# Carrying a hand-made instruction order across the seam between two graph-attention layers

## The chip, the cores and the metric

The kernel runs on one core of one Trainium2 chip. The metric is the device time of one execution in microseconds (us). Before the change three timed runs gave 937.43, 938.22 and 939.72 us; their median is 938.22 us. The profile below comes from one further execution, of 938.49 us, whose profiled span is 936.6 us.

## The reference: what is computed

Two layers work on 4096 nodes with 512 features. `x` is (4096, 512), `adj` is (4096, 4096) with about one entry in some hundreds above zero. Each layer is a layer norm, a ReLU and an attention, added to its input. Layer 0 attends only inside blocks of 128 nodes; layer 1 attends over all edges, with eight heads.

```python
# layer 0: attention inside each graph of 128 nodes, biased by adj
h = jnp.maximum(_layernorm(x), 0.0)
query, key, value = h @ Wq.T + bq, h @ Wk.T + bk, h @ Wv.T + bv
a = jnp.where(mask, query @ key.T * scale, 0.0)
scores = (a + adj + adj) * jnp.where(mask, 1.0, -1000000.0)
x = x + (jax.nn.softmax(scores, axis=-1) * mask) @ value

# layer 1: every node attends over its neighbours, 8 heads of 64
h = jnp.maximum(_layernorm(x), 0.0)
mx = jnp.einsum('nf,hfd->hnd', h, W)
logits = s_i[:, :, None] + t_j[:, None, :]      # s = mx.a_origin, t = mx.a_dst
attn = jax.nn.softmax(jnp.where(adj[None] > 0, logits, neg_inf), axis=-1)
x = x + concat_heads(einsum('hij,hjd->hid', attn, mx))
```

The kernel works on 32 row tiles of 128 nodes. It has three stages. Stage one is layer 0: 16 iterations of two row tiles each, `g = 0` to `15`. Stage two, the part between the layers, finishes for every row tile `i` the layer norm and ReLU of layer 1, turns the tile (features to partitions), multiplies it with `W` and weighs it with `exp(t)`; the result is `parts[i]`. Part of this is already done inside stage one: row tiles 0 to 7 are projected there, and row tiles up to 15 are normed and turned there. Stage three is layer 1's aggregation, one long product of the 0/1 mask with the 32 parts for each of 32 row tiles.

## The kernel before

The constants that matter are `NT = 32` row tiles, `G = 2` tiles an iteration, `NG = 16` iterations, `LO = 8`, `AHEAD = 10`, `BY = 4` row tiles in a chunk, and `KC = 4`. A "chunk" of four row tiles is turned in two steps: the vector engine transposes blocks of 32 by 32 into a buffer `blocks`, the buffer is stored to memory (`store`), and it is read back with the features on the partitions (`move`). The buffers of the helpers' results come from pools with a fixed number of buffers; `ps_p` has four PSUM buffers, and every projection takes two of them.

The helpers of one row tile `i` of layer 1 are these:

```python
def moments(src):                                    # two DVE and two POOL operations
    nc.vector.bn_stats(stats, src)
    nc.vector.bn_aggr(mv, stats)
    nc.gpsimd.tensor_scalar(ve, mv[:, 1:2], EPS, None, ALU.add)
    nc.gpsimd.tensor_tensor(rstd, ve, neghalf, ALU.pow)
    return mv[:, 0:1], rstd

def norm(src, hn, of=None):                          # one DVE operation
    mean, rstd = of or moments(src)
    nc.vector.tensor_scalar(hn, src, mean, rstd, ALU.subtract, ALU.mult)

def turn(i, row, pool):                              # one DVE operation
    c, b = divmod(i, BY)
    if b == 0:
        blocks[c] = pool.tile([P, P // B, KC, BY, B], F32, name="blocks")
    nc.vector.transpose(blocks[c][:, :, :, b], ...)

def store(c):                                        # 1 MB to memory
    nc.sync.dma_start(hT_d[c], ...blocks[c]...)

def move(c):                                         # 1 MB back, four DMAs
    hT = keep.tile(..., tag="a" if c and c % 2 == 0 else "hT4")
    for q in range(P // B):
        nc.sync.dma_start(hT[ts(q, B)]..., hT_d[c, :, q]...)

def fetch(i):                                        # pool sb2 has two of these buffers
    rows[i] = sb2.tile([P, D], F32, name="row1")
    nc.sync.dma_start(rows[i], x1_d[i])

def relu1(i):
    norm(rows[i], rows[i], of[i])
    nc.scalar.activation(rows[i], rows[i], AF.Relu)

def project1(ps_m, hT, w1x):                         # 16 matmul records, two PSUM buffers
    pm = [ps_m.tile([P, D], F32, name="pp") for _ in range(2)]
    for g, n in ((1, HW + H), (0, HW)):
        for k in range(KC):
            nc.tensor.matmul(pm[g][:, :n], hT[:, k, :], w1x[:, k, ...], ...)
    return pm

def prepare():
    i = len(parts)
    pm = project1(ps_p, hTs[i], w1x)
    e = weights(i, pm)                               # exp on ACT, two small POOL operations
    return lambda: finish(e, pm, part_tile(lo, i))   # two DVE products (weigh), a cast on ACT,
                                                     # a subtraction on POOL (split)
```

The end of an iteration of stage one, its last iteration and the part between the layers are as follows.

```python
with tc.manual_schedule(engines={E.PE, E.DVE, E.Activation, E.Pool, E.SP}):
    for g in range(NG - 1):
        mine = g - 1
        # ... loads, scores, queries, masks ...
        if g > 1:
            of[mine] = moments(rows[mine])
        if g:
            fetch(g)
        # ... values of the next pair ...
        attend(sT, vs[0], g, 0, lambda: nvs.append(v0()))   # a matmul, x1 = ... on DVE, x1 stored
        attend(sT, vs[1], g, 1)
        if g:
            relu1(mine)
        # ...
        nvs.append(values(nhT, 1))
        if g:
            turn(mine, rows[mine], keep)
        # ...

    g = NG - 1
    fetch(g)
    s = scores(hT, gT, rs[g], *look)
    rest = prepare()
    of[g - 1] = moments(rows[g - 1])
    row_sums(g, *look)
    relu1(g - 1)
    sT = turned(s)
    turn(g - 1, rows[g - 1], keep)
    rest()
    rest = prepare()
    of[g] = moments(rows[g])
    relu1(g)
    attend(sT, vs[0], g, 0)
    rest()
    rest = prepare()
    turn(g, rows[g], keep)
    store(LO // BY + 1)
    attend(sT, vs[1], g, 1)
    rest()

# ... pools of layer 0 closed, pools hi and sb4p opened ...

with tc.manual_schedule(engines={E.DVE, E.Activation, E.Pool, E.SP}):
    first = LO + AHEAD
    for i in range(2 * LO, first + 2):
        load(i)                                      # sb4, five buffers "row2"
    move(LO // BY + 1)
    for i in range(2 * LO, first):
        norm(rows[i], rows[i])
        nc.scalar.activation(rows[i], rows[i], AF.Relu)
        if i + 1 < first:
            turn(i, rows[i], keep)
    for i in range(LO, NT):
        far = i + AHEAD
        load(far + 2)
        if far % BY == 1 and LO + AHEAD < far <= NT + 1:
            move(far // BY - 1)
        # ... first mask of stage three, near the end ...
        low()
        if far < NT:
            of[far] = moments(rows[far])
        if far <= NT:
            turn(far - 1, rows[far - 1], ...)
            if far % BY == 0:
                store(far // BY - 1)
        pm = project1(ps_p, hTs[i], w1x)
        if before:
            low = finish(*before, later=True)
        if far < NT:
            norm(rows[far], rows[far], of[far])
        before = (weights(i, pm), pm, upper[i])
        if far < NT:
            nc.scalar.activation(rows[far], rows[far], AF.Relu)
```

Inside `manual_schedule` the named engines take their instructions in the order of the program. There are two such contexts here, one after the other, and the second does not name PE. Where the two meet, the framework's own scheduler decides how the instructions of one are mixed with those of the other: in the profile the loads of row tiles 16 to 19 stand on the queue at 325.81 us, ahead of `fetch(15)` at 335.57 us, which the program has first.

Of the kernel before, what the change touches and what calls it, by code (L numbers as in the profile page):

```python
# [9 lines left out]
F32 = mybir.dt.float32  # L10
# [43 lines left out]
def kernel(  # L54
# [332 lines left out]
    with ExitStack() as straight:  # L387
# [4 lines left out]
        with ExitStack() as prep:  # L392
# [26 lines left out]
            def store(c):  # L419
                nc.sync.dma_start(hT_d[c], blocks[c].rearrange("p q k b r -> p q (k b r)"))  # L420
# [13 lines left out]

            rows, of = {}, {}

            def fetch(i):
                rows[i] = sb2.tile([P, D], F32, name="row1")
                nc.sync.dma_start(rows[i], x1_d[i])

            def relu1(i):
# [22 lines left out]
            with (  # L464
# [90 lines left out]
                def store_mask(i):  # L555
                    nc.sync.dma_start(a_d[i], a8s[i].bitcast(F32))
# [9 lines left out]
                def seen():  # L566
                    return (
                        sb.tile([P, G, P], F32, name="diag"),
                        [small.tile([P, 4], F32, name="sums", bufs=8) for _ in range(G)],
                        [],  # L570
                    )
# [45 lines left out]
                def load_pair(g):  # L617
                    xg[g] = sb.tile([P, G, D], F32, name="xg", bufs=3)
                    nc.sync.dma_start(
                        xg[g], x[g * G * P : (g + 1) * G * P, :].rearrange("(t p) d -> p t d", p=P)  # L620
                    )
# [35 lines left out]


                E = mybir.EngineType
                with tc.manual_schedule(engines={E.PE, E.DVE, E.Activation, E.Pool, E.SP}):  # L660
                    for g in range(NG - 1):
                        new = G * (g + 1)
                        mine = g - 1
                        if g + 2 < NG:
                            load_pair(g + 2)
                        if g in (5, 9, 13):
                            store(g // BY - 1)
                        if g == 1:
                            fetch(0)
                            w1x, dots = load_w1(pool1, sb2, tag="e")  # L670
                        if g in (6, 11, 14):
                            move((6, 11, 14).index(g))
                        nlook = seen()

                        def look_on(t, h):
                            sum_half(new + t, h, nlook[0][:, t, :], nlook[1][t], nlook[2])

                        def between(m):
                            if m < 2:
                                mask_half(new, m)  # L680
                                look_on(0, m)
                            if m == 1:
                                store_mask(new)
                                row_sums(g, *look)
                            if m > 1:
                                mask_half(new + 1, m - 2)

                        s = scores(hT, gT, rs[g], *look)
                        ngT = queries(nhT, between)
                        sT = turned(s)  # L690
                        if g + 2 < NG:
                            ofs = [moments(xg[g + 2][:, t, :]) for t in range(G)]
                        look_on(1, 0)
                        rest = prepare() if g in (7, 8, 9, 10, 13) else None
                        look_on(1, 1)
                        store_mask(new + 1)
                        if g > 1:
                            of[mine] = moments(rows[mine])
                        if g:
                            fetch(g)  # L700
                        if g + 2 < NG:
                            hns = normed0(g + 2, ofs)
                        if 2 <= g < 2 + KC:
                            dots(g - 2)
                        v0 = values(nhT, 0, later=True)
                        nvs = []
                        if rest:
                            rest()
                        attend(sT, vs[0], g, 0, lambda: nvs.append(v0()))
                        attend(sT, vs[1], g, 1)  # L710
                        if g == 1:
                            of[0] = moments(rows[0])
                        if g:
                            relu1(mine)
                        if g + 2 < NG:
                            rs[g + 2] = row_terms(hns)
                        nvs.append(values(nhT, 1))
                        if g:
                            turn(mine, rows[mine], keep)
                        hT, gT, vs, look = nhT, ngT, nvs, nlook  # L720
                        if g + 2 < NG:
                            nhT, hns = turned0(g + 2, hns)


                    g = NG - 1
                    fetch(g)
                    s = scores(hT, gT, rs[g], *look)
                    rest = prepare()
                    of[g - 1] = moments(rows[g - 1])
                    row_sums(g, *look)  # L730
                    relu1(g - 1)
                    sT = turned(s)
                    turn(g - 1, rows[g - 1], keep)
                    rest()
                    rest = prepare()
                    of[g] = moments(rows[g])
                    relu1(g)
                    attend(sT, vs[0], g, 0)
                    rest()
                    rest = prepare()  # L740
                    turn(g, rows[g], keep)
                    store(LO // BY + 1)
                    attend(sT, vs[1], g, 1)
                    rest()

# [11 lines left out]
                    rows[i] = sb4.tile([P, D], F32, name="row2", bufs=5)  # L759
                    nc.sync.dma_start(rows[i], x1_d[i])  # L760

            E = mybir.EngineType
            with tc.manual_schedule(engines={E.DVE, E.Activation, E.Pool, E.SP}):
                first = LO + AHEAD
                for i in range(2 * LO, first + 2):
                    load(i)
                move(LO // BY + 1)
                for i in range(2 * LO, first):
                    norm(rows[i], rows[i])
                    nc.scalar.activation(rows[i], rows[i], AF.Relu)  # L770
                    if i + 1 < first:
                        turn(i, rows[i], keep)
                before = None
                low = lambda: None
                for i in range(LO, NT):
                    far = i + AHEAD
                    load(far + 2)
                    if far % BY == 1 and LO + AHEAD < far <= NT + 1:
                        move(far // BY - 1)
                    if far == NT + 1:  # L780
# [12 lines left out]
                    low()  # L793
                    if far < NT:
                        of[far] = moments(rows[far])
                    if far <= NT:
                        turn(far - 1, rows[far - 1], (keep, sb4)[(far - 1) // BY % 2])
                        if far % BY == 0:
                            store(far // BY - 1)
# [393 lines left out]
```

## Time and profile before

| what | from the page |
|---|---|
| span | 936.6 us |
| PE (matmul) busy | 922.0 us |
| DVE busy | 475.0 us |
| ACT busy | 261.4 us |
| POOL busy | 161.1 us |
| mean granted TensorE clock | 0.995 |
| stage one, from the first matmuls to the last scores | until about 336 us |
| part between the layers | about 336 to 442 us |
| stage three, aggregation | 442 us to the end |

PE stands for the matrix engine, DVE for the vector engine, ACT for the scalar engine, POOL for the general-purpose engine and SP for the queue engine that issues most transfers. A busy PE only says that matmuls are in flight. The boundaries of the stages are read from the chain of waits, in which the products of line 322 (stage three) start at 442.08 us and the last scores of line 578 at 334.20 us. Line 271 is the projection of the part between the layers, line 280 the weighing that frees its PSUM buffers, line 415 the block transpose of `turn`, line 420 the store of a chunk, line 428 its way back, line 612 the `x1` of layer 0's attention and line 760 the load of a row tile.

### The profile page before, as it was taken

How to read it: one execution, taken by the hardware profiler on the slowest of the kernel's cores; microseconds unless marked ns; L12 is line 12 of the kernel's file. 1: busy time of each engine (PE TensorE's matmuls, PEld its weight loads, DVE VectorE, ACT ScalarE, POOL GpSimd, SP SyncE). 2: the span in 40 equal slices, each digit the busy share in tenths (PEclk: the TensorE clock that was granted, in tenths of full speed). 3: DMA queues.
4: the chain of work that ended last, by engine and by line, in shares of the span. 5: the costliest groups of instructions: out<-in, count | busy, mean ns of one | idle time of the engine just before them, and what ended most of it. 6: DMA issues, size and time to landing. Idle time of an engine off the chain costs nothing.

```text
span 936.6 us, 13023 instructions
## 1 busy us (share of the span) xinstructions
PE 922.0 (98%) x4933; PEld 804.9 (86%) x4933; DVE 475.0 (51%) x1016; ACT 261.4 (28%) x507; POOL 161.1 (17%) x344
## 2 busy tenths in 40 slices
PE   8999999999999998999999999999999999999997
PEld 6776676767777666888999999999999999999997
DVE  5477888777677656645362424242423233232412
ACT  5476677655567633332000000000000000000000
POOL 2112111222211224554101011010101010101010
PEclk9999999999999998999999999999999999999999
DMA  9999999999899636762213131312222221312111
GB/s 340 409 330 390 367 378 363 366 377 350 307 346 366 211 131 173 222 177 66 68 46 91 46 91 51 85 51 85 54 82 69 68 86 50 90 46 91 45 45 37
DMA packets 63941, 165.01 MB, mean 176 GB/s; under 512 B 7042, under 2 KB 23810, under 8 KB 54658
## 3 DMA queue, kind: packets, MB, share of 16 engines
q1 hardware_dynamic: 54370, 147.35, 46.9%
q10 hardware_dynamic: 9504, 16.78, 4.7%
q8 instruction: 40, 0.66, 0.3%
q14 instruction: 27, 0.22, 0.1%
HBM read 122.16 MB, written 41.94 MB: 175 GB/s over the span
## 4 chain that ended last, share of the span: by engine, by line
PE 93%; DMA 3%; DVE 1%; POOL 1%; issue 0%; ACT 0%; SPq 0%; ACTq 0%; DVEq 0%
PE pg L322 51%; PE pp L504 12%; PE pp L517 12%; PE pp L271 8%; PE pss L578 3%; PE pp L609 3%; PE pt L135 1%; PE pp L242 1%; DMA row<-x_d 1%; PE pl L322 1%; DMA hT_d<-blocks 1%; DMA bk_sb<-bk 0%; POOL rstd L123 0%; PE pss L601 0%; DVE stats L117 0%
## 5 line engine op out<-in xcount | busy, mean ns | idle before, releaser
L322 PE MATMUL pg<-part,ata 128*128 128x348 f32 (+1 forms) x1536 | 246.8, 321 | 0.0
L322 PEld LDWEIGHTS pg<-part,ata 128*128 128x128 f32 x1536 | 244.5, 188 | 0.1
L322 PE MATMUL pg<-part,atb 128*128 128x348 f32 x1472 | 236.8, 321 | 0.0
L322 PEld LDWEIGHTS pg<-part,atb 128*128 128x128 f32 x1472 | 234.6, 188 | 0.1
L336 ACT COPY tot<-pg 128x522 f32<-128x522 f32 x31 | 18.5, 598 | 454.0 <-PE pg L322 454.0
L547 ACT ACTIVATE junk<-a 128x2048 bf16<-128x2048 f32 (+15 forms) x92 | 124.5, 1353 | 1.3
L271 PE MATMUL pp<-w1x,hT 128*128 128x256 f32 (+1 forms) x512 | 117.1, 389 | 6.0 <-DVE e L280 4.8
L271 PEld LDWEIGHTS pp<-w1x,hT 128*128 128x128 f32 x512 | 98.2, 194 | 23.4 <-issue 6.5
L517 PE MATMUL pp<-wv,hT 128*128 128x512 f32 x256 | 114.9, 592 | 0.0
L308 DVE CAST atb<-at 128x4096 fp32r<-128x4096 fp8e4 x16 | 36.7, 2294 | 152.6 <-PE pg L322 152.6
L504 PE MATMUL pp<-hT,m_sb 128*128 128x256 f32 x512 | 113.2, 379 | 0.0
L308 DVE CAST ata<-at 128x4096 fp32r<-128x4096 fp8e4 (+1 forms) x17 | 36.9, 2168 | 140.5 <-PE pg L322 140.4
L504 PEld LDWEIGHTS pp<-hT,m_sb 128*128 128x128 f32 x512 | 96.1, 190 | 12.9 <-issue 0.5
L517 PEld LDWEIGHTS pp<-wv,hT 128*128 128x128 f32 x256 | 47.9, 190 | 54.3 <-issue 53.8
L144 DVE TENSOR_SCALAR a<-a 128x512 fp8e4<-128x512 f32 x256 | 90.3, 447 | 1.2 <-DMA a<-adj 1.2
L844 POOL COPY den_all<-tot 128x1 f32<-128x1 f32 x31 | 5.7, 184 | 365.9 <-DVE tot L337 365.9
L848 POOL TENSOR_TENSOR tot<-tot,row 128x512 f32<-128x512 f32 x31 | 39.9, 1287 | 61.9 <-DVE tot L342 59.9
L121 POOL TENSOR_SCALAR ve<-mv 128x1 f32<-128x1 f32 x64 | 15.3, 239 | 193.9 <-DVE mv L119 193.9
L255 POOL TENSOR_TENSOR part<-e,part 128x522 fp32r<-128x522 f32 x32 | 40.7, 1272 | 15.1 <-ACT part L252 8.9
L123 POOL TENSOR_TENSOR rstd<-ve,neghalf 128x1 f32<-128x1 f32 x64 | 41.3, 645 | 5.3
L299 DVE STREAM_TRANSPOSE at<-mw 128x1024 f32<-128x1024 f32 x32 | 39.6, 1238 | 0.0
L523 DVE TENSOR_TENSOR v<-pp,bv_sb 128x512 f32<-128x512 f32 x32 | 22.0, 688 | 29.3 <-PE pp L517 29.3
(108 smaller groups left out, 661.7 us busy)
## 6 DMA issues: line engine op xcount, KB each, us to landing
a<-adj SPq DMA_DIRECT2D x64, 1024.0 KB, 8.7
a_d<-a SPq DMA_DIRECT2D x32, 512.0 KB, 9.4
row<-x_d SPq DMA_DIRECT2D x64, 256.0 KB, 3.7
mw<-a_d SPq DMA_DIRECT2D x128, 128.0 KB, 3.9
xg<-x SPq DMA_DIRECT2D x16, 512.0 KB, 10.6
x_d<-x ACTq DMA_DIRECT2D x32, 256.0 KB, 7.3
hT_d<-blocks SPq DMA_DIRECT2D x8, 1024.0 KB, 5.0
hT<-hT_d SPq DMA_DIRECT2D x32, 256.0 KB, 6.3
```

The lines of the kernel that those rows point to most:

```text
L123: nc.gpsimd.tensor_tensor(rstd, ve, neghalf, ALU.pow)
L144: nc.vector.tensor_scalar(a8v[:, u], av[:, u], 0.0, None, ALU.is_gt, saturate=False)
L255: nc.gpsimd.tensor_sub(dst[:, :, 1, :], e3, dst[:, :, 0, :].bitcast(F32))
L271: nc.tensor.matmul(pm[g][:, :n], hT[:, k, :], w1x[:, k, g * HW : g * HW + n], start=(k == 0), stop=(k == KC - 1),)
L299: nc.vector.transpose(at8.rearrange("p c n b -> p (c n b)").bitcast(F32).rearrange("p (c u n) -> p c u n", c=NW, n=B), mw.rearrange("p u ( ...
L308: nc.vector.tensor_copy(at[:, c0 * BY : c1 * BY].rearrange("p (c b) q -> p c b q", b=BY), at8[:, c0:c1].rearrange("p c q b -> p c b q"),)
L322: nc.tensor.matmul(pg[:, : 2 * CW1].rearrange("p (s w) -> p s w", s=2)[:, :, :n], at[:, j, :], part(j)[:, c, :, :n], start=(j == 0), stop= ...
L504: nc.tensor.matmul(pp[:, : G * P], m_sb[:, k, ts(m, P)], hT[:, k, :], start=(k == 0), stop=(k == KC - 1),)
L517: nc.tensor.matmul(pp, hT[:, k, ts(t, P)], wv[:, k, :], start=(k == 0), stop=(k == KC - 1))
L547: nc.scalar.activation(junk[:, c0:c1], a[:, c0:c1], AF.Exp, scale=2.0 * NEG, accum_out=sums[:, n : n + 1],)
L578: nc.tensor.matmul(pss[:, t, :], gT[:, k, ts(t, P)], hT[:, k, ts(t, P)], start=(k == 0), stop=(k == KC - 1),)
L848: nc.gpsimd.tensor_add(num, num, row)
```

## The change

The change keeps one hand-made context over the seam. The context is entered before stage one and left after the part between the layers, so PE is ordered by hand there too and no scheduler mixes the two programs. For this the seam is rearranged. In the last but one iteration (`g = 14`) no new input pair is prepared any more, so two `hn` buffers and one `xg` buffer are idle; row tiles 14 to 17 are fetched into them. Tiles 14 and 15 are normed and turned in that iteration, so that their chunk can be stored at the start of the last one; tiles 16 and 17 are normed and turned within the last iteration, between its own operations. The five buffers of the part between the layers are then loaded with tiles 18 to 22 at once. The purpose is that the last iteration's own work and the tiles that the projection waits for come in a chosen order.

The diff follows, with changes of mere indentation left out.

```diff
-            def fetch(i):
-                rows[i] = sb2.tile([P, D], F32, name="row1")
+            def fetch(i, to=None):
+                rows[i] = sb2.tile([P, D], F32, name="row1") if to is None else to
                 nc.sync.dma_start(rows[i], x1_d[i])
...
-                with tc.manual_schedule(engines={E.PE, E.DVE, E.Activation, E.Pool, E.SP}):
+                by_hand = ExitStack()
+                by_hand.enter_context(
+                    tc.manual_schedule(engines={E.PE, E.DVE, E.Activation, E.Pool, E.SP})
+                )
                 for g in range(NG - 1):
...
+                    if g == NG - 2:
+
+                        for i in (g, g + 1):
+                            fetch(i, sb.tile([P, D], F32, name="hn"))
+                        more = sb.tile([P, G, D], F32, name="xg", bufs=3)
+                        for t in range(G):
+                            fetch(g + 2 + t, more[:, t, :])
                     if g in (6, 11, 14):
                         move((6, 11, 14).index(g))
...
                     if g > 1:
                         of[mine] = moments(rows[mine])
-                    if g:
+                    if 0 < g < NG - 2:
                         fetch(g)
+                    if g == NG - 2:
+                        of[g], of[g + 1] = moments(rows[g]), moments(rows[g + 1])
...
+                    if g == NG - 2:
+                        relu1(g)
+                        relu1(g + 1)
+                        turn(mine, rows[mine], keep)
                     nvs.append(values(nhT, 1))
-                    if g:
-                        turn(mine, rows[mine], keep)
+                    for i in (g, g + 1) if g == NG - 2 else (mine,) if g else ():
+                        turn(i, rows[i], keep)
...
                 g = NG - 1
-                fetch(g)
+                store(LO // BY + 1)
                 s = scores(hT, gT, rs[g], *look)
                 rest = prepare()
-                of[g - 1] = moments(rows[g - 1])
+                for i in (2 * LO, 2 * LO + 1):
+                    of[i] = moments(rows[i])
                 row_sums(g, *look)
-                relu1(g - 1)
                 sT = turned(s)
-                turn(g - 1, rows[g - 1], keep)
                 rest()
                 rest = prepare()
-                of[g] = moments(rows[g])
-                relu1(g)
-                attend(sT, vs[0], g, 0)
+                for i in (2 * LO, 2 * LO + 1):
+                    relu1(i)
                 rest()
+                attend(sT, vs[0], g, 0)
+                for i in (2 * LO, 2 * LO + 1):
+                    turn(i, rows[i], keep)
                 rest = prepare()
-                turn(g, rows[g], keep)
-                store(LO // BY + 1)
-                attend(sT, vs[1], g, 1)
                 rest()
+                attend(sT, vs[1], g, 1)
...
-            E = mybir.EngineType
-            with tc.manual_schedule(engines={E.DVE, E.Activation, E.Pool, E.SP}):
-                first = LO + AHEAD
-                for i in range(2 * LO, first + 2):
+            with by_hand:
+                ahead = LO + AHEAD + 5
+                for i in range(LO + AHEAD, ahead):
                     load(i)
                 move(LO // BY + 1)
-                for i in range(2 * LO, first):
-                    norm(rows[i], rows[i])
-                    nc.scalar.activation(rows[i], rows[i], AF.Relu)
-                    if i + 1 < first:
-                        turn(i, rows[i], keep)
...
-                    load(far + 2)
+                    if far + 2 >= ahead:
+                        load(far + 2)
...
-                    if far <= NT:
+                    if LO + AHEAD < far <= NT:
                         turn(far - 1, rows[far - 1], (keep, sb4)[(far - 1) // BY % 2])
```

## The prediction

> **What bounds the kernel now.** I read the page first, then the list of waits of PE, then PE's timeline around the seam, then the chain of waits, then a table of windows.
>
> ```profile
> PE 922.0 (98%) x4933; PEld 804.9 (86%) x4933; DVE 475.0 (51%) x1016; ACT 261.4 (28%) x507; POOL 161.1 (17%) x344
> ...
> PEclk9999999999999998999999999999999999999999
> ```
>
> PE is busy for 922.0 of 936.6 us: the kernel is bound by PE, and only 14.6 us of idle PE can be won at all. Slice 16 (351 to 375 us) is the only one in which the granted clock falls.
>
> ```profile
> PE pp L271 <- DVE e L280: 4.8, 2, 4.6
> PE pt L198 <- POOL ident masks.py:199: 1.5, 1, 1.5
> PE pp L271 <- DVE x L612: 1.2, 1, 1.2
> ```
>
> The columns are total, times and longest. Of the 14.6 us some 8 lie at the start, before the first matmuls; the change does not touch them. The seam has 4.8 + 1.2 = 6.0 us: one wait of 1.2 on the `x1` of the last layer-0 iteration, one of 4.6 on a weighing, and one of 0.2.
>
> ```profile
> 343.91 1.94 PE L271 MATMUL pp<-w1x,hT 128*128 128x264 f32 x8
> 347.07 1.99 PE L271 MATMUL pp<-w1x,hT 128*128 128x256 f32 x8 [1.22 <-DVE x L612]
> 348.90 1.02 PE L609 MATMUL pp<-v,sT 128*128 128x512 f32 x2
> 349.76 7.18 PE L271 MATMUL pp<-w1x,hT 128*128 128x264 f32 x32
> 361.53 34.49 PE L271 MATMUL pp<-w1x,hT 128*128 128x264 f32 x144 [4.59 <-DVE e L280]
> 396.26 3.97 PE L271 MATMUL pp<-w1x,hT 128*128 128x264 f32 x17 [0.24 <-DVE e L280]
> ```
>
> PE projects row tile 7 in two halves, the second late; then tiles 8 and 9; then it stands still until tile 8's PSUM buffers are free. The row of 144 has a second loss. A projection of 16 matmuls takes 3.51 us in the chain (0.219 each), so 144 should take 31.6 us; they took 34.5. The missing 2.9 us are a slow clock:
>
> ```profile
> 360.00:361.00 1.00, 0.00 (x0) 0.00 (x0) 0.96 (x4) 0.33 (x1) 0.35 (x2) 0.54 1.06 211
> ...
> 365.50:366.50 1.00, 1.00 (x4) 0.73 (x4) 0.97 (x3) 0.68 (x2) 0.78 (x2) 0.50 1.12 410
> 366.50:367.50 1.00, 1.00 (x5) 0.86 (x4) 0.73 (x2) 0.00 (x0) 0.92 (x3) 0.80 0.87 205
> ```
>
> The third number from the end is the granted clock: half speed from 360 to about 367 us, four matmuls per us instead of between four and five. (5.4 us of work at half clock are 2.7 lost, which agrees with the 2.9.)
>
> Why the weighing was late stands in the chain of waits:
>
> ```profile
> 347.68 0.63 DVE blocks L415
> 348.32 5.85 DMA hT_d<-blocks
> 354.27 0.71 DVE blocks L415
> 354.98 0.59 DVE stats L117
> 356.17 0.58 POOL rstd L123
> ```
>
> Tile 15 is turned only at 347.68; its chunk goes to memory in 5.85 us; the next `turn`, of tile 16, needs the same buffer and holds DVE until 354.27. Behind it in DVE's order stand the moments, norm and turn of tiles 17 and 18, and only then, at 361.00, the weighing of tile 8, which had been ready since about 353.5 (its projection ended 3.5 us after 349.76).
>
> [...] 4.6 us of idling, then half clock; the return took 5.4 us of work here. So removing a wait of 4.6 us is worth more than 4.6. [...] DVE stood idle 2.89 us before the turn of tile 16 with the moments of tile 17 behind it. [...] I take only the measured 5.85 and the median of the stores around here, 4.4 us.
>
> **The change part by part.** Durations are those of the timeline: statistics 0.69 and aggregation 0.18 on DVE; 0.22 and 0.57 on POOL; norm 0.55; turn 0.70; two weighing products of 0.4.
>
> (a) Iteration 14 gets two more tiles. DVE adds 2 × (0.87 + 0.55 + 0.70) = 4.2 us. Its timeline has the room: it idles 3.43 us before the values' addition at 329.08, where the moments fit, and 2.23 us before the one at 334.23, where the two extra norms fit (1.1 us) with the turn of tile 13. Only the turns of 14 and 15 come after 334.92; they end at 336.2 instead of one turn at 335.5. The scores' step on DVE then starts at 336.2 instead of 336.02; PE needs its result only after 339.3. Cost on PE: nothing. The four fetches wait for the `hn` buffers (transposes end 316.5) and land, at 3.7 to 5.5 us each, by about 323, before the moments at about 325.5.
>
> (b) The chunk of tiles 12 to 15 is stored at about 336.3 instead of 348.32, and has landed by 340.7 to 342.2. Tile 16 is turned after the first `x1`, at about 344.8. The 2.89 us wait on DVE and the chain behind it are gone.
>
> (c) In the last iteration, tile 6's weighing comes before the first `x1`, and the norms of 16 and 17 before both. Walking DVE: moments of 16 and 17 until 338.1, row sums 338.7, weighing of tile 5 until 339.9, two norms until 341.0, weighing of tile 6 when its matmuls end at 343.05, until 343.7, `x1` from 344.1 (its matmuls end at 343.9) to 344.85. Before, `x1` began at 346.27, behind two norms that waited on POOL. Tile 7's projection starts at 343.9 and by the order in which buffers come free it takes those of tiles 5 and 6. So the 1.22 us go.
>
> (d) PE then runs tile 7 to 347.4, the second attention to 348.3, tile 8 to 351.8, tile 9 to 355.3, and wants tile 8's buffers. DVE: weighing of 7 to 348.0, second `x1` 348.45 to 349.2, moments of 18 to 350.0, idle about 1.1 us for POOL, norm of 18, moments of 19, turn of 18 to 353.1, weighing of 8 from 353.1, first half free at 353.5. That is 1.8 us before PE asks. Afterwards DVE needs about 0.87 + 0.70 + 0.75 + 0.55 = 2.9 us a tile against PE's 3.51, so it gains. The 4.59 and the slow clock's 2.9 go.
>
> (e) Tiles 18 to 22 are loaded from 336.6 on, `move` of chunk 3 follows when tile 7 has freed its buffer (347.4), and tile 12 is wanted only at 362.4. From tile 23 on the loads keep the old order: behind `move`, which waits for PE to finish a chunk. This left waits of 0.17 (at 381.7) and 0.24 us in the old trace and should leave about the same, perhaps 0.4 in all.
>
> Sum: 1.2 + 4.6 + 2.9 = 8.7 us off, the small waits kept. 938.2 − 8.7 = 929.5; I allow 0.4 for a small new wait and say 929.9.
>
> **The rivals.** First: a new wait takes the old one's place. Most exposed is (d), DVE's walk to the weighing of tile 8, because the first tile gets no head start; if ACT's cast into the first `hi` buffer must await the store of an `x1` under it (4.0 us to landing), ACT falls behind and tile 9's weighing slips to about 359 against PE's 358.8. For it: it is a single strict order now, with nobody to fill a hole. Against it: 1.8 us of slack. It would leave 1 to 3 us: 931 to 933. [...]
>
> Second: the steady balance. With 4.6 us of delay gone, DVE may meet the row loads (6.46 us in the chain, DVE idle 3.45 at 379.79) with less in hand, and each of three or four chunks may give 0.3 to 1 us back: 931 to 933. Against it: those loads are released by PE's own progress, so the distances do not shrink with an earlier start.
>
> Third: iteration 14's extra 4.2 us of DVE, or fetches landing late, delay stage one. DVE has 3.43 + 2.23 us of holes there, so I give it little; 1 us at most.
>
> Fourth: the slow clock does not come from the wait. Then 2.9 us stay and the time is 932.5. It came exactly behind the only long wait, so I think this unlikely.
>
> **Range and chances.** PE's work is untouched and stage three is wholly PE, so the gain cannot exceed 1.2 + 4.6 + 0.2 + 2.9 = 8.9 us: 929.3, less about 1 for the spread of the runs. That gives the low end 928.0. The rivals one and two together put the high end at 934.0. Two per cent is 18.8 us, more than twice all that can be won; a loss of 18.8 would need a failure I see no sign of.
>
> **What would show it.** Right: PE's list of waits has neither `x` of line 612 nor 4.6 us of `e` of line 280; granted clock 1.00 from 330 to 442; line 322 begins at about 433.4 instead of 442.08; the store of chunk 3 at about 336.3. Wrong: a wait of PE above 1 us between 336 and 360, a clock below 1 there, or DVE idle on row loads with PE idle behind it. The prediction fails if line 322 begins later than about 438.

## The result, and the profile after

Six runs of the changed kernel gave a median of 930.99 us (929.46 to 933.17), beside 938.57 us for six runs of the kernel before (937.43 to 940.10). The ratio is 0.992, with a 95% interval of 0.9902 to 0.9937: faster by 0.8%, within two per cent. The profiled execution took 930.15 us, its span is 928.3 us against 936.6.

The page's first lines, the same as were shown of before:

```profile
PE 919.4 (99%) x4933; PEld 803.4 (87%) x4933; DVE 474.3 (51%) x1016; ACT 261.1 (28%) x507; POOL 160.8 (17%) x344
...
PEclk9999999999999999999999999999999999999999
```

PE has the same 4933 instructions and was busy for 2.6 us less, since in the seam none of them ran in a slow clock (granted clock 1.00 from 330 to 434 us; before, it was 0.66 from 360 to 370); the 8 in its clock row is gone. The rest of the 8.3 us is idle PE: 936.6 − 922.0 = 14.6 before, 928.3 − 919.4 = 8.9 after. The list of PE's waits says where (total, times, longest):

```profile
PE pt L198 <- POOL ident masks.py:199: 1.5, 1, 1.5
PE pp L609 <- DVE e L280: 0.8, 1, 0.8
PE pt L205 <- DMA wkT_sb<-wkT: 0.4, 1, 0.4
PE pp L271 <- DVE e L280: 0.3, 1, 0.3
```

The 1.2 on `x` of line 612 and the 4.6 on `e` of line 280 are gone. A wait of 0.8 on line 609 is new to this list; it lies in stage one, and the experiments come back to it. PE's timeline over the seam:

```profile
334.96 1.95 PE L578 MATMUL pss<-hT,gT 128*128 128x128 f32 x16
336.74 3.67 PE L271 MATMUL pp<-w1x,hT 128*128 128x264 f32 x16
...
343.98 1.02 PE L609 MATMUL pp<-v,sT 128*128 128x512 f32 x2
344.84 3.67 PE L271 MATMUL pp<-w1x,hT 128*128 128x264 f32 x16
348.34 1.02 PE L609 MATMUL pp<-v,sT 128*128 128x512 f32 x2
349.20 38.87 PE L271 MATMUL pp<-w1x,hT 128*128 128x264 f32 x176
388.36 45.83 PE L271 MATMUL pp<-w1x,hT 128*128 128x264 f32 x208 [0.29 <-DVE e L280]
433.84 6.40 PE L322 MATMUL pg<-part,ata 128*128 128x348 f32 x38
```

Tile 7's projection is one piece again, and 176 matmuls follow without a gap. From the last scores (334.96) to the first product of stage three (433.84) the seam takes 98.88 us. The same two lines of before:

```profile
334.03 1.95 PE L578 MATMUL pss<-hT,gT 128*128 128x128 f32 x16
...
441.73 8.47 PE L322 MATMUL pg<-part,ata 128*128 128x348 f32 x51
```

Before it took 441.73 − 334.03 = 107.70, so it is 8.82 us shorter now. (442.08, the number given for the start of stage three before, is from the chain of waits, which lets a product begin 0.35 us later than the timeline does. In the chain the seam takes 107.88 and 99.07 us, 8.81 less. The expectations below still count from 442.08 − 334.03 = 108.05, which mixes the two views.) In this execution stage one ended 0.93 us later than in the one shown of before, and what follows the seam took 0.4 us less, so the span gained 8.3. The seam's length is the measure for all the runs below, because it leaves stage one's chances out.

DVE's and SP's timeline of the changed kernel shows why PE found its buffers:

```profile
337.09 0.33 SPq L420 DMA_DIRECT2D hT_d<-blocks  x1
...
345.04 0.75 DVE L612 SCALAR_TENSOR_TENSOR x<-pp,rs_all,xg 128x512 f32<-128x512 f32 x1 [0.43 <-PE pp L609]
...
345.70 1.30 DVE L415 STREAM_TRANSPOSE blocks<-xg 128x512 f32<-128x512 f32 x2
...
353.85 0.72 DVE L280 TENSOR_TENSOR e<-pp,e 128x256 f32<-128x256 f32 x2
```

Chunk 3 goes to memory at 337.09 instead of 348.32. The first `x1` starts 0.2 us after its matmuls end, the turns of tiles 16 and 17 wait for nothing, and tile 8 is weighed at 353.85 instead of 361.00. PE asks for the first of its buffers at 356.2 (349.20 plus 32 matmuls of 0.219).

### The profile page after: what moved, and what is told of

Same layout as the page of the kernel before. It is cut to its first block, busy times and chain, and to the rows that moved or that the text cites. A ratio compares the mean times of both kernels' runs of the same rounds, so it can differ in the third digit from the quotient of the medians.

```text
span 928.3 us, 13021 instructions
## 1 busy us (share of the span) xinstructions
PE 919.4 (99%) x4933; PEld 803.4 (87%) x4933; DVE 474.3 (51%) x1016; ACT 261.1 (28%) x507; POOL 160.8 (17%) x344
## 4 chain that ended last, share of the span: by engine, by line
PE 90%; DMA 6%; DVE 1%; ACT 1%; POOL 1%; issue 0%; SPq 0%; DVEq 0%; ACTq 0%
PE pg L322 52%; PE pp L517 10%; PE pp L504 10%; PE pp L271 9%; PE pss L578 3%; PE pp L609 3%; DMA xg<-x 2%; PE pp L242 1%; DMA row<-x_d 1%; PE pt L135 1%; DMA x_d<-x 1%; PE pl L322 1%; DMA a<-adj 1%; DMA hT_d<-blocks 0%; DMA bk_sb<-bk 0%
## 5 line engine op out<-in xcount | busy, mean ns | idle before, releaser
L271 PE MATMUL pp<-w1x,hT 128*128 128x256 f32 (+1 forms) x512 | 114.1, 383 | 0.3 <-DVE e L280 0.3
L280 DVE TENSOR_TENSOR e<-pp,e 128x256 f32<-128x256 f32 x64 | 25.1, 411 | 27.0 <-PE pp L271 13.7
```

The source lines that it names most:

```text
L271: nc.tensor.matmul(pm[g][:, :n], hT[:, k, :], w1x[:, k, g * HW : g * HW + n], start=(k == 0), stop=(k == KC - 1),)
```

## The experiments

All times are medians; the kernel before, run beside each group, stood at 938.3 to 939.1 us. The four terms to be told apart are the early store of chunk 3, the early tiles 16 and 17, the one context (no mixing by the scheduler), and the clock.

| run | what | seam, us | time, us | ratio to before, 95% interval |
|---|---|---|---|---|
| (before) | | 107.7 | 938.3 to 939.1 | |
| (after) | | 98.9 | 930.99 | 0.9902 to 0.9937 |
| c0 | after, again | 98.5 | 931.47 | 0.9913 to 0.9950 |
| e1 | before, own buffer for chunk 4 | 107.2 | 937.62 | 0.9983 to 1.0012 |
| e2 | before, PE kept at work in the hole | 104.3 | 935.47 | 0.9962 to 0.9984 |
| e4 | before's order, one context | 109.5 | 941.96 | 1.0030 to 1.0061 |
| e3 | after's order, two contexts | 99.3 | 930.94 | 0.9892 to 0.9934 |
| e5 | after, chunk 3 stored late | 103.6 | 935.82 | 0.9945 to 0.9975 |
| e8 | e5, own buffer for chunk 3 | 102.1 | 933.67 | 0.9920 to 0.9962 |
| e12 | after, tiles 16 and 17 not early | 106.9 | 938.84 | 0.9984 to 1.0006 |
| e9 | after, loads on ACT's queue | 103.1 | 935.48 | 0.9956 to 0.9999 |
| e11 | after, chunk 0 read back later | 98.6 | 937.58 | 0.9974 to 0.9993 |
| e10 | after, tile 0 weighed first | 99.1 | 930.09 | 0.9893 to 0.9921 |
| e13 | e10, row loads ahead of the read-back | 98.2 | 928.88 | 0.9867 to 0.9913 |

**c0, the changed kernel again.**

> The changed kernel itself, for a second profile. Measure used in all runs: the seam, from the start of the last layer-0 scores on PE (line 578) to the first product of line 322; it was 108.05 us before and 98.88 us after. Every theory: seam 98.9 again. What is open: the changed kernel's profile had one PE wait of 0.8 us in stage one, behind a late xg transfer, which the kernel before had not. If this is chance of the transfers, another profile has another wait there or none, and the time moves by about that; if it comes from the change, the same wait of 0.8 us stands in the same iteration again.

The seam repeats. The wait of stage one repeats in place (iteration 7), but with 1.67 us instead of 0.78. Over the first ten profiles it was 0.7 to 1.9 us in five, one of them (e2) built from the kernel before, and 0.3 or none in the others. Up to iteration 13 the two kernels have the same program, and e2 shows that the wait comes without the change too. But it stood in one of four profiles of the old order, and in all six of the new order that left this part as it was (0.3 to 1.9 us, e12 among them). Whether the change makes it likelier is open.

**e1, the shared buffer taken away from the kernel before.**

```diff
-                        turn(i, rows[i], keep)            # tiles 16, 17
+                        turn(i, rows[i], sb4)
...
-                        turn(far - 1, rows[far - 1], (keep, sb4)[(far - 1) // BY % 2])
+                        turn(far - 1, rows[far - 1], (sb4, keep)[(far - 1) // BY % 2])
```

> The kernel before with one thing undone: chunk 4 is turned into the other pool's blocks buffer, so that the turn of tile 16 need not await the store of chunk 3. Nothing is fetched or turned earlier. Theory A (the chain through the store holds DVE[...]): the 2.9 us wait of DVE on the store is gone, the weighing of tile 8 comes about 2.9 us earlier, PE's 4.6 us wait falls to about 1.7, the clock stays at 1.00, so 2.9 + 2.9 = 5.8 us are won: seam 102.3, about 932.8 us. Rival B (the store is hidden: tile 8's weighing waits for the row loads and for the mixed order of the two contexts anyway): PE's wait stays above 4 us, clock falls as before, seam above 107.

A miss for both. The weighing of tile 8 did come 2.5 us earlier (358.50 instead of 361.00), as theory A had it, and yet only 0.5 us of the seam went. DVE's timeline of this run shows what happened first:

```profile
347.03 0.71 DVE L415 STREAM_TRANSPOSE blocks<-row 128x512 f32<-128x512 f32 x1 [0.70 <-ACT row L770]
347.67 0.71 DVE L612 SCALAR_TENSOR_TENSOR x<-pp,rs_all,xg 128x512 f32<-128x512 f32 x1
348.29 0.74 DVE L280 TENSOR_TENSOR e<-pp,e 128x256 f32<-128x256 f32 x2
...
363.80 0.69 DVE L117 BATCH_NORM_STATS2 stats<-row 128x6 f32<-128x512 f32 x1 [4.13 <-DMA row<-x_d]
```

With two contexts the scheduler, no longer held back by the store, put tile 16's turn (347.03) ahead of the first `x1` (347.67, was 346.27). PE's wait on `x1` grew from 1.22 to 2.60 us, one of 2.27 on a weighing followed at 365.76 instead of the 4.59, and the clock fell after each (0.50 from 350 to 352 us and from 367 to 369). The second has a cause that theory A had not: the next row loads were issued only from 357.30 on, behind the late store and the read-back (`move`) that awaits it, and DVE stood 4.13 us on them ahead of tile 9's weighing. The hole moved; it was not filled.

**e2, PE kept at work in the hole of the kernel before.**

```diff
+                    if i == LO + 2:
+                        pt = ps_t.tile([P, KC, P], F32, name="pt")
+                        for _ in range(36):
+                            nc.tensor.transpose(pt[:, 0, :], ident, ident)
                     pm = project1(ps_p, hTs[i], w1x)
```

> The kernel before with 36 transposes of the identity (0.109 us each, 3.9 us) on PE between the projections of tiles 9 and 10, into a PSUM buffer that is idle there. They compute nothing that is used. They keep PE at work in the hole and make no other engine faster. Theory A (the slow clock is the wait's consequence): the granted clock stays 1.00, the 144 matmuls behind the hole take 31.6 us instead of 34.5, seam 105.2, about 935.7 us, although tile 8's weighing is as late as before. Rival C (the clock falls for another reason, such as the burst of work on the other engines): clock 0.5 for some 7 us again, seam 108 or more.

PE's timeline and its clock over the same stretch (third number from the end of the second fence):

```profile
350.96 7.18 PE L271 MATMUL pp<-w1x,hT 128*128 128x264 f32 x32
357.97 4.09 PE L803 MATMUL pt<-ident 128*128 128x128 f32 x36
362.31 7.92 PE L271 MATMUL pp<-w1x,hT 128*128 128x264 f32 x35 [0.24 <-DVE e L280]
```

```profile
358.00:362.00 4.00, 4.00 (x37) 3.83 (x35) 3.55 (x9) 1.33 (x3) 1.53 (x6) 1.00 1.05 217
362.00:366.00 4.00, 3.76 (x18) 3.27 (x18) 3.43 (x9) 1.73 (x4) 2.45 (x7) 1.00 0.54 203
```

Tile 10's projection starts 11.35 us after tile 8's (362.31 − 350.96), before it was 11.77 (361.53 − 349.76): nearly as late. But the clock stays at 1.00, and the time falls by 2.8 us with work that nobody uses. The slow clock was the wait's consequence, and theory A's 2.9 us for it stands. (The seam is 3.4 us shorter: 0.4 of that is the shorter hole, 0.2 the later wait of 0.24, which is missing here, and 2.8 the clock.)

**e4, the old order in one context.** The order of the program is the old one.

```diff
-                with tc.manual_schedule(engines={E.PE, E.DVE, E.Activation, E.Pool, E.SP}):
+                by_hand = ExitStack()
+                by_hand.enter_context(tc.manual_schedule(engines={E.PE, E.DVE, E.Activation, E.Pool, E.SP}))
+                if True:
...
-            E = mybir.EngineType
-            with tc.manual_schedule(engines={E.DVE, E.Activation, E.Pool, E.SP}):
+            with by_hand:
```

> The kernel before in its old order, but with one hand-made context over the seam that names PE too, as in the changed kernel: no scheduler mixes the two programs. No early fetch, chunk 3 stored as late as its place in the program. Theory A (late chunk 3 is what counts): the 1.2 us wait on x1 goes, the store starts at about 346 and tile 16 is turned behind it, PE still waits about 4 us for tile 8's buffers and the clock falls: seam 106 to 108, 936 to 938 us. Rival D (the scheduler's mixing was the fault): both waits shrink to below 1.5 us and the clock stays, seam below 102, 932 us or less.

Worse than before by 0.3 to 0.6% (the seam by 1.8 us), a miss for both theories. The wait on `x1` went as foreseen (1.22 to 0.20), but in the program's order the loads of tiles 16 to 19 stand on SP behind the store of chunk 3, and the scheduler had moved them 22 us ahead of it. DVE stood 2.74 us on them, and PE for 7.58:

```profile
PE pp L271 <- DVE e L280: 7.6, 1, 7.6
PE pt L198 <- POOL ident masks.py:199: 1.5, 1, 1.5
PE pp L271 <- DVE x L612: 0.2, 1, 0.2
```

**e3, the new order with the scheduler let in again.**

```diff
-            with by_hand:
+            by_hand.close()
+            with tc.manual_schedule(engines={E.DVE, E.Activation, E.Pool, E.SP}):
```

> The changed kernel with its fetches and its order, but with two hand-made contexts again, the second without PE, so that the scheduler may mix the two programs at the seam. Theory A (the early fetch and store do it alone): seam 99 to 99.5 us, 931 us. Revised theory E, after the two runs in which only one of the two was taken (each of them gave nothing): both are needed; mixed in, the moments and norms of tiles 18 and 19 come ahead of the weighings and of the second x1, PE gets a wait of 0.5 to 2.6 us again, seam 100 to 103.5, 932 to 935 us.

Theory A was right and the revised one fell. The scheduler does mix: DVE takes the moments of tile 18 before the row sums, and its norm between tile 5's two weighings. But the rows are there and DVE has slack, so PE keeps working; its only wait behind the last scores is 0.79 us at 389, on row loads. Seam 99.3 us: of the 8.8 us at most 0.4 belong to the one context.

**e5 and e8, chunk 3 late again.** In e5 tile 15 is turned, and chunk 3 stored, after the first `x1`; in e8 chunk 3 has a buffer of its own besides.

```diff
-                    for i in (g, g + 1) if g == NG - 2 else (mine,) if g else ():
+                    for i in (g,) if g == NG - 2 else (mine,) if g else ():
...
                 g = NG - 1
-                store(LO // BY + 1)
...
                 attend(sT, vs[0], g, 0)
+                turn(g, rows[g], keep)
+                store(LO // BY + 1)
# e8 only, in turn():
-                    blocks[c] = pool.tile([P, P // B, KC, BY, B], F32, name="blocks")
+                    blocks[c] = (adj0 if c == 3 else pool).tile(
+                        [P, P // B, KC, BY, B], F32, name="a" if c == 3 else "blocks"
+                    )
```

> The changed kernel with tile 15 turned only after the first x1 of the last iteration, and chunk 3 stored behind that, as late as in the kernel before; fetches, one context and all else as changed. Tile 16's turn then has to await the store (4.4 to 5.9 us) in the same buffer. Theory A and E: DVE stands at that turn from about 347.5 to 352, the weighing of tile 7 and the second x1 come behind it, PE waits about 3 us for buffers in tile 8 and loses clock: seam 102.5 to 105.5, 934.5 to 937 us. Rival F (with the rows already in SBUF the late store is hidden): seam below 100.

> The run with the late store, and chunk 3 turned in an idle adjacency buffer, so that tile 16's turn awaits nothing. The store is as late as there. Theory A and E (it is the shared buffer, not the lateness of the data): seam back to 98.9 to 99.6, 931 us, since tile 12 is wanted only some 12 us after the store has landed. Rival G (the late chunk itself delays the projection of tiles 12 to 15): PE waits at tile 12, seam above 101.

e5 is as theory A has it; DVE's timeline shows the turn of tile 16 held back for 5.80 us:

```profile
348.29 0.70 DVE L415 STREAM_TRANSPOSE blocks<-hn 128x512 f32<-128x512 f32 x1
354.79 1.31 DVE L415 STREAM_TRANSPOSE blocks<-xg 128x512 f32<-128x512 f32 x2 [5.80 <-DMA hT_d<-blocks]
356.02 0.72 DVE L280 TENSOR_TENSOR e<-pp,e 128x256 f32<-128x256 f32 x2
```

The late store costs 103.6 − 98.9 = 4.7 us. Taking the buffer conflict away gave back only 1.5 of them, so e8 is a miss. The trace puts the other 3.2 us down to SP's order. The loads of tiles 18 to 22 stand behind the late store, issue from 346.60 instead of 337.51, and take 7.25 us to issue instead of 3.53:

```profile
346.18 0.33 SPq L422 DMA_DIRECT2D hT_d<-a  x1
346.60 7.25 SPq L778 DMA_DIRECT2D row<-x_d  x5
352.64 0.69 DVE L117 BATCH_NORM_STATS2 stats<-row 128x6 f32<-128x512 f32 x1 [2.74 <-DMA row<-x_d]
```

DVE starts tile 18 at 352.64 and stays behind: PE waits 0.84 us at tile 10, then 1.76 and 0.61 (tiles 15 and 19) as the next row loads come, 3.2 us in all. Rival G's place (tile 12) was wrong as well. No run has the loads ahead of a late store, so what each of the two costs alone is not shown; in e5 the wait for the buffer covers the one for the rows.

**e12, tiles 16 and 17 not early.** Their fetch in iteration 14 and their moments, norms and turns in iteration 15 are taken out; they stand after the last iteration as in the kernel before. All in one context.

```diff
-                        more = sb.tile([P, G, D], F32, name="xg", bufs=3)
-                        for t in range(G):
-                            fetch(g + 2 + t, more[:, t, :])
...
-                for i in (2 * LO, 2 * LO + 1):          # moments, relu1 and turn in iteration 15
-                    of[i] = moments(rows[i])            # (three such loops)
...
-                ahead = LO + AHEAD + 5
-                for i in range(LO + AHEAD, ahead):
+                first = LO + AHEAD
+                ahead = first + 3
+                for i in range(2 * LO, ahead):
                     load(i)
                 move(LO // BY + 1)
+                for i in range(2 * LO, first):
+                    norm(rows[i], rows[i])
+                    nc.scalar.activation(rows[i], rows[i], AF.Relu)
+                    turn(i, rows[i], keep)
```

> The changed kernel with tiles 14 and 15 early and chunk 3 stored early, in one context, but tiles 16 and 17 not fetched early: they are loaded with tiles 18 to 20 and normed and turned after the last iteration, as in the kernel before. Theory H (what counts is work taken off DVE's way between the second x1 and tile 8's weighing): the two tiles put some 6 to 8 us of serial DVE and POOL work there, PE waits 4 to 6 us in front of tile 10 and loses clock: seam 105.5 to 108.5, 936 to 939 us. Rival (the early store of chunk 3 is the whole gain): seam below 101, 932 us or less.

Theory H holds: PE waits 5.48 us, and the early store alone is worth nothing in time against the kernel before (it is 2.6 us of the seam against e4, the old order in one context). DVE's timeline between the second `x1` and tile 8's weighing is a serial chain with a hole at each norm (POOL) and each turn (ACT):

```profile
352.37 0.55 DVE L129 TENSOR_SCALAR row<-row,mv,rstd 128x512 f32<-128x512 f32 x1 [1.00 <-POOL rstd L123]
353.61 0.71 DVE L415 STREAM_TRANSPOSE blocks<-row 128x512 f32<-128x512 f32 x1 [0.70 <-ACT row L776]
...
356.10 0.55 DVE L129 TENSOR_SCALAR row<-row,mv,rstd 128x512 f32<-128x512 f32 x1 [0.98 <-POOL rstd L123]
357.34 0.71 DVE L415 STREAM_TRANSPOSE blocks<-row 128x512 f32<-128x512 f32 x1 [0.69 <-ACT row L776]
...
361.73 0.72 DVE L280 TENSOR_TENSOR e<-pp,e 128x256 f32<-128x256 f32 x2
```

From 350.47 to 357.98 it is 7.5 us for the two tiles. In one context the four corners are thus: neither 109.5 (e4), chunk 3 early 106.9 (e12), tiles 16 and 17 early 103.6 (e5), both 98.9. Each alone leaves a wait after which the clock fell to 0.50 (5.48 us in e12, 2.73 in e5).

**e9, the loads on ACT's queue.** The layer-0 pairs (from the third on) and the row loads of the part between the layers are issued by ACT instead of SP.

```diff
-                    nc.sync.dma_start(xg[g], ...)
+                    (nc.scalar if g > 1 else nc.sync).dma_start(xg[g], ...)
...
-                    nc.sync.dma_start(rows[i], x1_d[i])      # row2
+                    nc.scalar.dma_start(rows[i], x1_d[i])
```

> The changed kernel with the loads of the layer-0 pairs (from the third on) and the row loads of the part between the layers issued from ACT's queue instead of SP's, where they stand behind transfers that wait. What is left in the changed kernel's profiles are a PE wait of 0.8 or 1.7 us in stage one behind a late xg, and one of up to 0.3 us on row loads. If their place on the queue is the cause: both waits below 0.2, DVE's waits on xg (16 us in all) and on row loads much shorter, 0.5 to 1.5 us less, 929.5 to 930.5 us, seam 98.6. Rival: the issues (0.35 us each) hold up ACT's exponentials in stage one, and PE waits more: 931 us or more.

A miss, nearer to the rival, though not where it looked for it. The wait of 0.8 in iteration 7 was gone, but in the seam PE waited 2.93 us and lost clock (0.50 from 361 to 363 us). Two lines of ACT's and DVE's timeline show the cause, and a third what it delayed:

```profile
350.95 2.65 ACTq L775 DMA_DIRECT2D row<-x_d  x5
355.37 0.69 DVE L117 BATCH_NORM_STATS2 stats<-row 128x6 f32<-128x512 f32 x1 [4.83 <-DMA row<-x_d]
...
359.16 0.72 DVE L280 TENSOR_TENSOR e<-pp,e 128x256 f32<-128x256 f32 x2
```

In ACT's order the loads of tiles 18 to 22 stand behind the last iteration's own work, and they were issued from 350.95 on instead of 337.51. DVE stood 4.83 us on the first of them, and tile 8 was weighed at 359.16 instead of 353.85. Issuing the five also kept ACT for 2.65 us ahead of tile 8's exponential, which came at 353.66, still before that row had landed. The two moves were made together, so the run does not say what the pairs alone would bring.

**e10 and e11, the wait of iteration 7.** In the profiles up to here DVE waits 3.6 to 5.9 us in iteration 7 for the layer-0 pair, and tile 0's weighing, which PE wants, stands behind the pair's norms. e10 changes DVE's order there, e11 moves the read-back of chunk 0, on which SP stood still in iteration 6, to the end of that iteration.

```diff
# e10
-                    if g + 2 < NG:
+                    if g + 2 < NG and g != 7:
                         ofs = [moments(xg[g + 2][:, t, :]) for t in range(G)]
...
                     store_mask(new + 1)
+                    if g == 7:
+                        rest()
+                        rest = None
+                        ofs = [moments(xg[g + 2][:, t, :]) for t in range(G)]
# e11
-                    if g in (6, 11, 14):
+                    if g in (11, 14):
                         move((6, 11, 14).index(g))
...
                     if 0 < g < NG - 2:
                         fetch(g)
+                    if g == 6:
+                        move(0)
```

> The changed kernel; in iteration 7 alone DVE weighs tile 0 before it takes the moments of the pair that comes late from memory. Five of ten profiles so far have a PE wait of 0.7 to 1.9 us there, two more 0.3 or 0.4 beside it, always behind that pair. If the wait is DVE's order there: no PE wait in iteration 7, 0.5 to 1.5 us less than the changed kernel, 929.5 to 930.5 us, seam unchanged at 98.6 to 98.9. Rival: the delay only moves to the norms that follow, and PE waits for the next pair's transposes instead; 931 us.

> The changed kernel; in iteration 6 the read-back of chunk 0 stands at the end of SP's order instead of near its start, where SP stood still until the chunk's store had landed (from 151.8 to 157.2 us). If that standstill is why the pair of iteration 7 is issued late: DVE's wait for that pair falls from 5.4 to 5.9 us to under 3, no PE wait in iteration 7, 929.5 to 930.5 us. Rival: chunk 0 is then late for its own projection in iteration 7 and PE waits there; or the pairs are late because the transfers are at their limit, and nothing changes, 931 us.

e10: the wait of PE on the weighing is gone (0.2 us on the transposed pair is left), stage one ends at 334.29, close to the 334.03 of the shown profile of before, and the four runs lie between 929.68 and 930.59, closer together than any of the changed kernel. e11 hit its rival: the chunk is late for its own projection, and DVE's wait for the pair grew to 7.4 us.

```profile
PE pp L271 <- DMA hT<-hT_d: 5.7, 1, 5.7
```

**e13, the row loads ahead of the read-back.**

```diff
-                    if far % BY == 1 and LO + AHEAD < far <= NT + 1:
+                    if (far % BY == 3 and LO + AHEAD + 1 < far < NT) or far == NT + 1:
                         move(far // BY - 1)
```

> The run with tile 0 weighed first, and in the part between the layers the read-back of chunks 4 to 6 placed two tiles later in SP's order, behind the loads of two more row tiles, which until now stood still behind it until PE had finished a chunk. Theory: DVE's two waits of some 3 us on row loads go, and with them the last PE wait of 0.3 to 0.8 us in front of the third chunk (0.8 and 0.6 in the last profiles); seam 98.3, 929.5 us, which is 0.3 to 0.6 less than without it. Rival: the read-back is then late itself and PE waits for its chunk; seam above 99, 931 us.

PE's list of waits over the whole kernel, and its timeline from tile 8 to stage three:

```profile
PE pt L198 <- POOL ident masks.py:199: 1.5, 1, 1.5
PE pp L504 <- ACT hT L136: 0.3, 1, 0.3
PE pt L205 <- ACT w L206: 0.2, 1, 0.2
```

```profile
348.75 84.32 PE L271 MATMUL pp<-w1x,hT 128*128 128x264 f32 x384
432.72 7.51 PE L322 MATMUL pg<-part,ata 128*128 128x348 f32 x45
```

All 384 matmuls of tiles 8 to 31 run in one piece, and DVE's waits on row loads (6.5 us in two pieces in the changed kernel) are gone. With 928.88 us this version is the fastest of all; its lead over e10 and the changed kernel shows in the traces and in the medians, but the intervals of the ratios overlap.

## Why the prediction was right

The time, 929.9 predicted and 930.99 measured, is within the range; the seam gained 8.82 us where the sum said 8.7. Line 322, put at about 433.4, began at 434.19 in the same view (the chain of waits), which is 433.3 if one takes off the 0.93 us that stage one ended later. By its steps:

(a) Iteration 14's extra work cost PE nothing. The turns of 14 and 15 ended at 337.05, and the scores' step on DVE began at 336.98; on the prediction's time axis, 0.93 us earlier, that is 336.1 and 336.05, where it said 336.2.

(b) The store was put at 336.3 and came at 337.09 − 0.93 = 336.2. But the only harm of the late store that the step named is the 2.89 us wait for the shared buffer, with the chain behind it. e1 shows that this wait alone, taken from the kernel before, is worth at most a fraction of a per cent. e8 shows that a late store still costs 3.2 us of seam when nothing waits for the buffer, and its trace puts that down to the row loads behind the store on SP. The mechanism named was one of two.

(c) The first `x1` was put at 344.1 and came at 345.04 − 0.93 = 344.1; the 1.22 us went. That the mixing of the two programs was to blame for it holds for the old order only (e1, e4). In the new order mixing is harmless (e3).

(d) This was the step that carried the time, and it was right. The weighing of tile 8 was put at 353.1 and came at 353.85 − 0.93 = 352.9; the slack, 1.8 us, was 1.9. So the sum is not luck, though (b) had only a part of the mechanism. e12 shows what carries it: the two tiles' 7.5 us of serial work is out of that walk.

(e) The small wait on row loads stayed, 0.29 us here, none in c0, and 0.58 to 0.79 in e10 and e3. The cause named, the loads behind `move`, is shown for DVE's waits on the rows, which e13 takes away with the order (6.7 us in e10); PE's small wait goes with them there, but c0 had none either.

The clock term, 2.9 us, is confirmed by e2. Shorter waits than that of before (4.59 us) lost clock too: e5 had a granted clock of 0.50 after 1.94 us.

Three readings were off, and nothing rested on them. Of the idle PE outside the seam 2.6 us lie in the first 30 us and 6.0 at the end of the span; the first matmul starts at 1.52. The windows of before count three to four matmuls a us at half clock and six to seven at full (367 to 371 us), not four and between four and five. And 929.3 less 1 is 928.3, not 928.0.

The difference of 1.1 us between the time and the prediction is of the size of the stage-one wait, which the sum had not. It was not in the one profile that the prediction could see, it varies from run to run, and e10, which takes it away, came to 930.09. That the whole difference is due to it is argued from these numbers, not shown; the kernel before can have this wait too (e2).

## What to carry to other kernels

Where a bound engine hands over between two stages, walk the helper engine's program order from its last duty to the next buffer that the bound engine asks for, and take whole items off that walk; freeing one buffer or fixing one order alone only moved the hole here. Look for transfers that are ready but stand in an issuing queue behind one that waits: moving them ahead cost nothing measurable here and took away both of DVE's waits on rows (e13). An idle stretch of the matrix engine can be worth more than its length: here 4.59 us of it cost about 2.8 us more in the slow clock behind it (e2), and 1.94 us were once followed by half clock (e5).

## What the runs showed of the hardware

The clock fell after shorter waits than the 4.59 us of before. PE's waits of 1.94 us (e5, stage one), 2.60 and 2.27 (e1), 2.73 (e5) and 2.93 (e9) were each followed by half clock; 1.67 (c0) and 1.76 (e8) were not. The windows of e5's first case show it:

```profile
186.00:188.00 2.00, 0.86 (x3) 0.03 (x1) 1.86 (x6) 0.00 (x0) 1.83 (x7) 1.00 1.02 320
188.00:190.00 2.00, 1.20 (x3) 0.72 (x4) 2.00 (x5) 0.63 (x1) 1.19 (x4) 0.95 1.00 414
190.00:192.00 2.00, 2.00 (x3) 0.72 (x3) 2.00 (x5) 0.51 (x1) 1.11 (x1) 0.50 1.00 422
192.00:194.00 2.00, 2.00 (x4) 0.76 (x3) 0.76 (x4) 0.12 (x1) 0.53 (x2) 0.69 1.02 429
```

PE is at work again from 188.8 on, and by the mean clocks of these windows it ran at one half from about 189.8 to 193.2. By the mean clocks of such windows the stretches of half clock lasted 3.4 us in e5 and e1 (each twice) and in e9, 6.8 after the waits of 4.59 (before) and 5.48 (e12), 10.2 after the 7.58 of e4, but again 3.4 after the 5.73 of e11: about once, twice and three times the same length.

The wait's length alone did not decide how long the half clock lasted. Of the 6.8 us of half clock PE was idle for the first 1.45 (before) and 1.72 us (e12), of the 10.2 for some 5.2 (e4), of the 3.4 in e11 for about 0.4. Why the stretches have these lengths, and what decides after how much idling the clock falls, was not shown: these are readings of single executions, and no run varied the wait alone.
